# Layer 1 of a two-layer convolution: silu on pairs of units over 128 partitions, residual rows loaded in the layout of the output, and another division of r between VectorE and ScalarE

## The chip, the cores and the metric

The kernel runs on one core of one Trainium2 chip. The metric is the device time of one execution in microseconds; the time before is the median of three runs, and lower is better. A core has TensorE (PE in the profile, its weight loads PEld), VectorE (DVE), ScalarE (ACT), GpSimd (POOL) and SyncE (SP, which here only issues DMAs).

## The reference

The input x has shape (4, 16, 256, 256): four images of 16 channels. Both layers have the form x = x + f(groupnorm(x)).

Layer 0 computes, for every pixel and channel, 25 logits by a 3x3 convolution, a softmax over them, and the sum of the 5x5 neighbourhood weighted by it. The change touches only what it prepares for layer 1.

Layer 1 is a convolution of spline features and of silu, both 3x3:

```python
base_w = base_weight.sum(axis=2)
spl_w = (spline_weight * spline_scaler[..., None]).sum(axis=2)
out = jnp.einsum('bjhwn,ijn->bihw', jax.nn.silu(patches), base_w)
out = out + jnp.einsum('bjhwns,ijns->bihw', bspl, spl_w)
out = out + bias_weight[None, :, None, None]
x = x + out
```

`bspl` are eight cubic B-spline bases of the normalised x. With the distance t of x from the centre of a basis, the kernel computes a basis as the difference of two clamped cubes: r = max(c - t, 0), s = r^2, s*r, and beside it (t - 2c)(c - t/2)^2, which `combine` clamps and adds.

## The kernel before

**Stages.** A prologue of some 110 us normalises the first image and prepares weights. Layer 0 then runs to about 2035 us, and layer 1 takes the rest. Layer 0 leaves its result in DRAM (`x1s`, one row of 256 values after the other for each channel), and layer 1 reads it from there.

**Units.** Layer 1 works through 64 units: 4 images times 16 bands of 16 image rows (`RU = 16`). For a unit n,

- `load_x(n)` (lines 1027 to 1034) brings 16 rows into one of three buffers `xta`, `xtb`, `xtc`, laid out over 128 partitions as 16 channels times 8 bases: two DMAs of 1 MB each;
- `load_tiles(n)` (line 1040) brings the same x into partitions 64 to 127 of one of three tiles `sla`, `slb`, `slc`: 4 DMAs (one per row offset d of `RD = 4`) to 16 partitions each, in rows of 1 KB;
- `distance`, `inner`, `square`, `cube`, `far`, `cubed`, `combined` (lines 1068 to 1108) make the features in chunks of four rows (`QR = 4`; 128x1024 elements) and write them into `ring`, which holds the rows of two units. `inner` makes r: chunks 0, 1 and 2 on VectorE (line 1079), the last four rows on ScalarE (a Relu, line 1077);
- `silu(n)` (line 1048) reads partitions 64 to 127 of the unit's `sl` tile and writes silu into partitions 0 to 63;
- `outputs(n)` (line 1225) accumulates in PSUM: 12 products (d, e) of `ring` with the spline weights `wt`, then 3 products of the `sl` tile with `ws`. `ws` holds the silu weights for partitions 0 to 63 and an identity for partitions 64 to 127, so the raw x of the upper half adds the residual;
- `put` (line 1210) adds the bias while it copies the PSUM sum to an SBUF tile `yo` on VectorE, and `store` issues two DMAs of 128 KB to the output. Both are two units behind (`LAG1 = 2`): in `features(n)` they handle unit n-2.

**Order.** `features(n)` (line 1168) writes out the order of the work by hand: it interleaves the later features of unit n with the earlier ones of unit n+1 (`ahead_of(n + 1)`) and with `distance` of unit n+2. `in_order` then chains all instructions of an engine in the order in which the code emits them, SP's DMAs too; nothing is reordered. In the steady stage the orders of one unit are, from `put` to `put`:

- DVE: put, cubed 2, cubed 3, combined 2, combined 3 (unit n), then inner 0 (n+2), cubed 0 (n+1), inner 1, combined 0, cubed 1, inner 2, combined 1, and the next put;
- ACT: far 3, distance, far 0, far 1, silu, square of chunks 0 and 1, relu, far 2, square of two rows, and the next far 3;
- SP: two stores (wait for put), load_x(n+3) (2 DMAs), a halo copy inside `ring` every other unit, load_tiles(n+2) (4 DMAs).

`far` writes a PSUM tile of a pool of two, so a `far` waits for the `combined` of two chunks before. Every second unit below 32 also runs one step of `scales`, a chain of small instructions for the normalisation of images 2 and 3.

Of the kernel before, what the change touches and what calls it, by code (L numbers as in the profile page):

```python
# [11 lines left out]
F32 = mybir.dt.float32  # L12
# [22 lines left out]
def conv_preact_kernel(  # L35
# [72 lines left out]
    for k, d in enumerate((0, RD - 1)):  # L108
        nc.vector.reduce_sum(inside[:, k : k + 1], ident[:, d:P:RD], AX.X)
    nc.vector.tensor_scalar(inside, inside, -1.0, 1.0, ALU.mult, ALU.add)  # L110
# [17 lines left out]

    ws = const.tile([P, 3, RT, C], F32, name="ws")
    nc.gpsimd.memset(ws, 0.0)  # L130
    for r in range(RT):
        nc.sync.dma_start(ws[P // 2 + r + 1 : P : RD, 1, r], ident[0:C, 0:C])

# [327 lines left out]
    with tc.tile_pool(name="prep0", bufs=2) as prep, tc.tile_pool(  # L461
# [98 lines left out]
        def prepare1():  # L560
# [18 lines left out]
            for r in range(RT):  # L579
                nc.vector.tensor_copy(  # L580
                    wt[:, r : r + 3, :, r, :], wcp.rearrange("p (d e o) -> p d e o", d=3, e=3)
                )
                for d in range(3):
                    nc.sync.dma_start(
                        ws[r + d : P // 2 : RD, :, r, :],
                        wb1[d * C : (d + 1) * C].rearrange("p (e o) -> p e o", e=3),
                    )

# [386 lines left out]
    def layer1(arm, last, marks, seeds):  # L975
# [5 lines left out]
        with ExitStack() as pools:  # L981
# [12 lines left out]
            xt0 = fixed("xta", XT)  # L994
            r1a, r1b = fixed("r1a", [P, 3 * QR, W])[0], fixed("r1b", [P, QR + 1, W], 2)
            s1a = fixed("s1a", XT)
# [5 lines left out]
            xtt = xt0 + xt1 + fixed("xtc", XT)  # L1002
            sl += fixed("slb", SL) + fixed("slc", SL)
            yop = pool("yo", 3)
            ps2 = pool("ps2", 2, space=PSUM)
# [34 lines left out]
            def load_tiles(n):  # L1040
                b, u = units[n]
                for d in range(RD):
                    nc.sync.dma_start(
                        sl[n % 3][P // 2 + d : P : RD, :, 1 : W + 1],
                        rows(x1s[b], [[CP, C], [RT * W, RU // RT], [1, W]], u * RU + d),
                    )

            def silu(n):
                b, u = units[n]
                q0, q1 = 1 if u == 0 else 0, RU // RT - (1 if u == NU - 1 else 0)  # L1050
                for a, z, k in ((0, q0, 4), (q0, q1, 0), (q1, RU // RT, 6)):
                    if a < z:
                        nc.scalar.activation(
                            sl[n % 3][0 : P // 2, a:z, 1 : W + 1],
                            sl[n % 3][P // 2 :, a:z, 1 : W + 1], AF.Silu,
                            scale=sc[b][k][P // 2 :], bias=sc[b][k + 1][P // 2 :],
                        )

            def r1(n, a, z):
                lo = span(units[n][1])[0]  # L1060
                t, o = (r1a, lo) if a - lo < 3 * QR else (r1b[n % 2], lo + 3 * QR)
                return t[:, a - o : z - o]
# [11 lines left out]
            def inner(n, a, z, act):  # L1074
                r, t = r1(n, a, z), xs(n, a, z)
                if act:
                    nc.scalar.activation(r, t, AF.Relu, bias=cb, scale=-1.0)  # L1077
                else:
                    nc.vector.scalar_tensor_tensor(  # L1079
                        r, t, cb, pc.unsqueeze(2).to_broadcast([P, z - a, W]), ALU.min, ALU.subtract  # L1080
                    )
# [21 lines left out]
            def combined(n, c, ps):  # L1103
                a, z = cuts(units[n][1])[c]
                combine(
                    ring[:, place(n) + a : place(n) + z, 1 : W + 1], ps, s1(n, a, z),
                    ALU.subtract if n > 0 and c < 3 else ALU.add,
                )

            def start_unit():  # L1110
                cs = cuts(0)
                for v in cs[:3]:
                    distance(0, *v)
                    inner(0, *v, True)
                    square(0, *v)
                    cube(0, v)
                    if v == cs[1]:
                        early = newest(POOLE).name
                v = cs[3][0], cs[-1][1]
                distance(0, *v)  # L1120
                inner(0, *v, True)
                square(0, *v)
                cube(0, *cs[3:])
                return early

            def ahead_of(n):
                cs = cuts(units[n][1])
                lo = cs[0][0]
                tail = cs[3][0], cs[-1][1]
                yield  # L1130
                inner(n, *cs[0], False)
                yield
                inner(n, *cs[1], False)
                yield
                square(n, lo, cs[1][1])
                cube(n, *cs[:2])
                inner(n, *tail, True)
                yield
                inner(n, *cs[2], False)
                yield  # L1140
                square(n, cs[2][0], lo + SQ)
                square_late(n, lo + SQ, cs[2][1])
                square_late(n, *tail)
                cube(n, *cs[2:])
                yield

            def first_features(ps):
# [11 lines left out]
                next(pre)  # L1159
                ps.append(far(0, 4))  # L1160
                silu(0)
                next(pre)
# [47 lines left out]
            def put(lag=LAG1):  # L1210
                if len(waiting) >= lag:
                    b, u, yp = waiting[0]
                    yo = yop.tile([P, 2, W], F32, name=f"yo_{b}_{u}{arm}", tag="yo")
                    nc.vector.tensor_scalar(yo, yp, bias_sb, None, ALU.add)
                    waiting[0] = b, u, yo
# [9 lines left out]
            def outputs(n):  # L1225
# [12 lines left out]
                for e in range(3):  # L1238
                    for t in range(NT):
                        nc.tensor.matmul(  # L1240
                            yp[t * M : (t + 1) * M],
                            lhsT=ws[:, e].rearrange("p r o -> p (r o)"),
                            rhs=sl[n % 3][:, t : t + NT + 1 : NT, e : e + W],
                            start=False, stop=e == 2,
                        )
# [7 lines left out]
            load_x(1)  # L1253
            load_tiles(0)
            load_x(2)
            load_tiles(1)
            def sides(t):
# [11 lines left out]
            halo(0)  # L1269
            for t in sl:  # L1270
                sides(t)
            first_far = [far(0, 0), far(0, 1)]
            first_rest = len(nc.cur_bb.bb.instructions)
            for n in range(len(units)):
                if n % 2:
                    next(more, None)
                if n > 0:
                    halo(n)
                    if n + 1 < len(units) and n > 0:
                        load_tiles(n + 1)  # L1280
                if n == 0:
# [3 lines left out]
                if n == 1:  # L1285
                    behind(seeds[2], newest(DVEE).name)
                if n + 3 < len(units):
                    load_x(n + 3)
                outputs(n)
            for _ in range(LAG1):  # L1290
                put(1)
                store(1)
# [61 lines left out]
```

## Time and profile before

| | us |
|---|---|
| median of 3 runs | 2939.93 (2938.02 to 2942.46) |
| the profiled execution's own time | 2938.03 |
| its span (first to last instruction) | 2936.3 |

| stage, us from the start of the span | length | PE | DVE | ACT | POOL | DMA share |
|---|---|---|---|---|---|---|
| 0 to 100 (prologue) | 100 | 46.24 | 71.22 | 69.85 | 35.41 | 0.93 |
| 1000 to 1500 (layer 0) | 500 | 477.78 | 495.56 | 330.35 | 488.35 | 0.85 |
| 2040 to 2100 (start of layer 1) | 60 | 51.02 | 55.31 | 54.82 | 50.59 | 0.65 |
| 2200 to 2800 (layer 1) | 600 | 594.86 | 597.35 | 594.08 | 545.67 | 0.70 |
| 2880 to 2936.3 (end) | 56.3 | 48.76 | 34.11 | 24.92 | 24.37 | 0.17 |

The columns of the engines are busy microseconds in the stage. A matmul's end is modelled, so a busy PE need not be one at its peak. DMA share is the mean busy share of the 16 DMA engines.

In a timeline a line gives start, duration, engine, line of the code, operation, output and input tiles, shape and count. Consecutive instructions of one engine overlap in their records by some 0.1 us, so the difference of two starts is the better price of an instruction. A strip of the DMA view cuts a window into 40 equal slices: the upper row is the busy share in tenths, the lower what was moved in GB/s.

The put of unit n-2 is a convenient mark of a unit. It starts at 2079.46 us in the first unit that has one, and 59 units later at 2883.95 us; most units take 13.52 us from put to put, the first of each image about 15.

### The profile page before, as it was taken

How to read it: one execution, taken by the hardware profiler on the slowest of the kernel's cores; microseconds unless marked ns; L12 is line 12 of the kernel's file. 1: busy time of each engine (PE TensorE's matmuls, PEld its weight loads, DVE VectorE, ACT ScalarE, POOL GpSimd, SP SyncE). 2: the span in 40 equal slices, each digit the busy share in tenths (PEclk: the TensorE clock that was granted, in tenths of full speed). 3: DMA queues.
4: the chain of work that ended last, by engine and by line, in shares of the span. 5: the costliest groups of instructions: out<-in, count | busy, mean ns of one | idle time of the engine just before them, and what ended most of it. 6: DMA issues, size and time to landing. Idle time of an engine off the chain costs nothing.

```text
span 2936.3 us, 40887 instructions
## 1 busy us (share of the span) xinstructions
PE 2742.2 (93%) x14282; PEld 1486.3 (51%) x14282; DVE 2840.3 (97%) x1866; ACT 2161.5 (74%) x2764; POOL 2703.7 (92%) x1116
## 2 busy tenths in 40 slices
PE   4699999999999899999999989996999999999998
PEld 3466656666666566656656656663323323222222
DVE  7599999999999999999999999998999999999996
ACT  6566876667766567667555554657999999999995
POOL 4399999999999999999999999999899999899895
PEclk7799999999999999999999999997999999999999
DMA  9988999889889788898886766766666767767663
GB/s 277 260 238 230 261 258 254 239 219 252 242 231 242 204 221 232 231 251 226 223 216 168 210 177 174 195 179 208 200 220 217 228 213 225 226 211 233 216 218 99
DMA packets 385736, 647.60 MB, mean 221 GB/s; under 512 B 41842, under 2 KB 250180, under 8 KB 369652
## 3 DMA queue, kind: packets, MB, share of 16 engines
q1 hardware_dynamic: 321556, 609.73, 73.4%
q10 hardware_dynamic: 61920, 31.46, 4.0%
q0 software_dynamic: 2048, 3.72, 0.5%
q8 instruction: 117, 1.92, 0.3%
q14 instruction: 95, 0.78, 0.1%
HBM read 516.18 MB, written 121.15 MB: 217 GB/s over the span
## 4 chain that ended last, share of the span: by engine, by line
DVE 39%; ACT 21%; PE 20%; DMA 8%; issue 7%; POOL 3%; SPq 2%; ACTq 0%; DVEq 0%; POOLq 0%
DVE nd L771 32%; PE lg L922 12%; ACT s L170 4%; PE lg L926 3%; PE yp L1231 3%; ACT xtc L1070 2%; ACT xtb L1070 2%; ACT xta L1070 2%; POOL e L950 2%; ACT s1a L1084 2%; DMA an<-hsl 2%; ACT s1b L1084 2%; ACT r1b L1077 1%; DMA am<-hst 1%; DVE ring L176 1%
## 5 line engine op out<-in xcount | busy, mean ns | idle before, releaser
L950 POOL TENSOR_TENSOR e<-e,u 128x1600 f32<-128x1600 f32 x512 | 1789.0, 3547 | 49.7 <-ACT e L945 49.4
L922 PE MATMUL lg<-wm,am 128*128 128x400 f32 x4096 | 1732.9, 504 | 74.3 <-ACT e L945 35.7
L771 DVE TENSOR_REDUCE nd<-e 128x128 f32<-128x3200 f32 x512 | 1762.9, 3494 | 30.3 <-POOL e L950 29.9
L926 PE MATMUL lg<-wn,an 97*128 97x400 f32 x2048 | 1342.5, 656 | 14.3 <-DMA an<-hsl 13.8
L945 ACT ACTIVATE e<-lg 128x800 f32<-128x800 f32 x1024 | 833.5, 838 | 577.2 <-PE lg L926 332.4
L922 PEld LDWEIGHTS lg<-wm,am 128*128 128x128 f32 x4096 | 763.5, 192 | 386.9 <-ACT e L945 64.4
L1231 PE MATMUL yp<-ring,wt 128*32 128x512 f32 x6144 | 763.5, 595 | 38.9 <-DVE ring L176 34.9
L926 PEld LDWEIGHTS lg<-wn,an 97*128 97x128 f32 x2048 | 387.4, 189 | 333.8 <-DMA an<-hsl 25.3
L1231 PEld LDWEIGHTS yp<-ring,wt 128*32 128x32 f32 x6144 | 223.1, 109 | 528.6 <-issue 421.9
L1091 POOL TENSOR_TENSOR s1a<-s1a,r1a 128x1024 f32<-128x1024 f32 x96 | 228.7, 2398 | 43.9 <-ACT s1a L1084 43.9
L1091 POOL TENSOR_TENSOR s1b<-s1b,r1a 128x1024 f32<-128x1024 f32 x96 | 228.9, 2400 | 35.1 <-ACT s1b L1084 35.1
L176 DVE SCALAR_TENSOR_TENSOR ring<-s,s1a 128x1024 f32<-128x1024 f32 x132 | 158.7, 1233 | 0.9
L825 ACT ACTIVATE z<-xc,nrm 128x256 f32<-128x256 f32 x240 | 144.0, 600 | 18.0 <-POOL xc L805 13.8
L176 DVE SCALAR_TENSOR_TENSOR ring<-s,s1b 128x1024 f32<-128x1024 f32 (+1 forms) x128 | 155.6, 1246 | 0.3
L173 DVE SCALAR_TENSOR_TENSOR s<-xta,cb,s 128x1024 f32<-128x1024 f32 (+2 forms) x90 | 113.6, 1293 | 0.7 <-ACT s L170 0.4
L173 DVE SCALAR_TENSOR_TENSOR s<-xtb,cb,s 128x1024 f32<-128x1024 f32 (+2 forms) x85 | 108.5, 1309 | 0.5 <-ACT s L170 0.4
L173 DVE SCALAR_TENSOR_TENSOR s<-xtc,cb,s 128x1024 f32<-128x1024 f32 (+2 forms) x85 | 108.2, 1305 | 0.4 <-ACT s L170 0.4
L170 ACT ACTIVATE s<-xta,cb 128x1024 f32<-128x1024 f32 (+2 forms) x90 | 96.5, 1086 | 7.4 <-DVE ring L176 7.0
L785 ACT ACTIVATE r<-nd 128x512 f32<-128x512 f32 x64 | 38.3, 598 | 78.9 <-DVE nd L799 78.9
L170 ACT ACTIVATE s<-xtc,cb 128x1024 f32<-128x1024 f32 (+2 forms) x85 | 91.8, 1094 | 1.3 <-DVE ring L176 0.7
L170 ACT ACTIVATE s<-xtb,cb 128x1024 f32<-128x1024 f32 (+2 forms) x85 | 91.8, 1093 | 0.8 <-DVE ring L176 0.4
L1079 DVE SCALAR_TENSOR_TENSOR r1a<-xtc,cb,pc 128x1024 f32<-128x1024 f32 x63 | 82.7, 1312 | 4.5 <-issue 4.5
(211 smaller groups left out, 2434.0 us busy)
## 6 DMA issues: line engine op xcount, KB each, us to landing
am<-hst SPq DMA_DIRECT2D x512, 194.6 KB
u<-hs SPq DMA_DIRECT2D x320, 288.0 KB
an<-hsl SPq DMA_DIRECT2D x512, 129.8 KB
xta<-x1s SPq DMA_DIRECT2D x40, 1024.0 KB
xtb<-x1s SPq DMA_DIRECT2D x40, 1024.0 KB
xtc<-x1s SPq DMA_DIRECT2D x40, 1024.0 KB
am<-hst SPq DMA_DIRECT2D x256, 129.8 KB
x1s<-xc ACTq DMA_DIRECT2D x30, 1024.0 KB
```

What stands on the lines that cost most here:

```text
L170: nc.scalar.activation(s, t, AF.Square, scale=-0.5, bias=cb)
L173: nc.vector.scalar_tensor_tensor(p, t, cb2, s, ALU.subtract, ALU.mult)
L176: nc.vector.scalar_tensor_tensor(f, p, 0.0, q, ALU.min, op)
L771: nc.vector.tensor_reduce(nd[:, :, :, j : j + JG].rearrange("p t c j -> p t j c"), e.rearrange("p t j m c d -> p t j c m d"), AX.XY, ALU.add,)
L825: nc.scalar.activation(z, v, f, scale=nrm[b][:, 0, g : g + 1], bias=nrm[b][:, 1, g : g + 1], accum_out=st1[b][:, t, g, columns_of(n) : col ...
L922: nc.tensor.matmul(lg[:, i, :NL], lhsT=am[:, o : o + P], rhs=wm.rearrange("p m c d -> p (m c d)"), start=True, stop=False,)
L926: nc.tensor.matmul(lg[:, i, :NL], lhsT=an[:, o : o + P], rhs=wn.rearrange("p m c d -> p (m c d)"), start=False, stop=True,)
L945: nc.scalar.activation(ev, lg[:, :, :NL], AF.Exp)
L950: nc.gpsimd.tensor_tensor(e[:, 1].rearrange("p j m c d -> p j (m c) d"), e[:, 0].rearrange("p j m c d -> p j (m c) d"), uv, ALU.mult,)
L1070: nc.scalar.activation(xs(n, a, z), xs(n, a, z), AF.Abs, scale=sc[b][2], bias=sc[b][3])
L1091: nc.gpsimd.tensor_tensor(s1(n, a, z), s1(n, a, z), r1(n, a, z), ALU.mult)
L1231: nc.tensor.matmul(yp[t * M : (t + 1) * M], lhsT=wt[:, d, e].rearrange("p r o -> p (r o)"), rhs=ring[:, r0 + t * RT + d : r0 + t * RT + d ...
```

## The change

It has four parts.

1. **silu of two units at a time.** Units 2m and 2m+1 share one `sl` tile: the even unit's x goes into partitions 0 to 63, the odd one's into 64 to 127. silu runs in place on all 128 partitions, in two halves of 1024 elements: the first in `features(2m-1)`, the second in `features(2m)`. `ws` becomes two sets of weights, one with zeros for the upper half and one with zeros for the lower; `outputs(n)` takes set n % 2. The identity in `ws` is gone.
2. **The residual in the layout of the output.** A new `load_rows(n)` loads the unit's 16 rows of x into the `yo` tile (two DMAs of 128 KB, each partition 1 KB), and `put` becomes one `scalar_tensor_tensor`: PSUM sum + bias + that tile, in place. The pool of `yo` has 4 buffers instead of 3.
3. **The order on SP.** After `features(n)`: load_tiles(n+3), load_x(n+3), load_rows(n-1), and then the next unit's halo. `put` in `features(n+1)` reads the rows that are loaded here.
4. **r for 10 rows on VectorE and the rest on ScalarE.** `inner` on VectorE makes 4 + 4 + 2 rows, the Relu on ScalarE six instead of four. r on VectorE changes its sign, so `combine` always adds. GpSimd's products follow the new cut: six rows squared in one instruction instead of two and four, and one chunk's cube in two halves.

In the prologue the two DMAs of the identity into `ws` (line 132) go, and the six DMAs of the silu weights (line 584) become twelve.

```diff
@@ prologue
-    ws = const.tile([P, 3, RT, C], F32, name="ws")
+    ws = const.tile([P, 2, 3, RT, C], F32, name="ws")
     nc.gpsimd.memset(ws, 0.0)
-    for r in range(RT):
-        nc.sync.dma_start(ws[P // 2 + r + 1 : P : RD, 1, r], ident[0:C, 0:C])
...
                 for d in range(3):
-                    nc.sync.dma_start(
-                        ws[r + d : P // 2 : RD, :, r, :],
-                        wb1[d * C : (d + 1) * C].rearrange("p (e o) -> p e o", e=3),
-                    )
+                    for h in range(2):
+                        nc.sync.dma_start(
+                            ws[h * (P // 2) + r + d : (h + 1) * (P // 2) : RD, h, :, r, :],
+                            wb1[d * C : (d + 1) * C].rearrange("p (e o) -> p e o", e=3),
+                        )
@@ layer1
-            r1a, r1b = fixed("r1a", [P, 3 * QR, W])[0], fixed("r1b", [P, QR + 1, W], 2)
+            r1a, r1b = fixed("r1a", [P, SQ, W])[0], fixed("r1b", [P, RU + 1 - SQ, W], 2)
...
-            yop = pool("yo", 3)
+            yop = pool("yo", 4)
...
             def load_tiles(n):
                 b, u = units[n]
+                h = n % 2 * (P // 2)
                 for d in range(RD):
                     nc.sync.dma_start(
-                        sl[n % 3][P // 2 + d : P : RD, :, 1 : W + 1],
+                        sl[n // 2 % 3][h + d : h + P // 2 : RD, :, 1 : W + 1],
                         rows(x1s[b], [[CP, C], [RT * W, RU // RT], [1, W]], u * RU + d),
                     )
 
+            def load_rows(n):
+                b, u = units[n]
+                t = yop.tile([P, 2, W], F32, name=f"yo_{b}_{u}{arm}", tag="yo")
+                for g in range(2):
+                    nc.sync.dma_start(
+                        t[:, g], rows(x1s[b], [[W, 8], [CP, C], [1, W]], u * RU + 8 * g + 1)
+                    )
+                kept_rows.append(t)
+
             def silu(n):
-                b, u = units[n]
-                q0, q1 = 1 if u == 0 else 0, RU // RT - (1 if u == NU - 1 else 0)
-                for a, z, k in ((0, q0, 4), (q0, q1, 0), (q1, RU // RT, 6)):
-                    if a < z:
-                        nc.scalar.activation(
-                            sl[n % 3][0 : P // 2, a:z, 1 : W + 1],
-                            sl[n % 3][P // 2 :, a:z, 1 : W + 1], AF.Silu,
-                            scale=sc[b][k][P // 2 :], bias=sc[b][k + 1][P // 2 :],
-                        )
+                m = (n + 1) // 2
+                if m >= len(units) // 2:
+                    return
+                b, u = units[2 * m]
+                q0, q1 = (0, RU // RT // 2) if n % 2 else (RU // RT // 2, RU // RT)
+                parts = [(q0, q1, 0)]
...
+                for a, z, k in parts:
+                    t = sl[m % 3][:, a:z, 1 : W + 1]
+                    nc.scalar.activation(t, t, AF.Silu, scale=sc[b][k], bias=sc[b][k + 1])
...
             def ahead_of(n):
...
                 square(n, lo, cs[1][1])
                 cube(n, *cs[:2])
-                inner(n, *tail, True)
+                inner(n, mid, hi, True)
                 yield
-                inner(n, *cs[2], False)
+                inner(n, cs[2][0], mid, False)
                 yield
-                square(n, cs[2][0], lo + SQ)
-                square_late(n, lo + SQ, cs[2][1])
-                square_late(n, *tail)
-                cube(n, *cs[2:])
+                square(n, cs[2][0], mid)
+                square_late(n, mid, hi)
+                cube_late(n)
                 yield
...
             def put(lag=LAG1):
                 if len(waiting) >= lag:
                     b, u, yp = waiting[0]
-                    yo = yop.tile([P, 2, W], F32, name=f"yo_{b}_{u}{arm}", tag="yo")
-                    nc.vector.tensor_scalar(yo, yp, bias_sb, None, ALU.add)
+                    yo = kept_rows.pop(0)
+                    nc.vector.scalar_tensor_tensor(yo, yp, bias_sb, yo, ALU.add, ALU.add)
                     waiting[0] = b, u, yo
...
             for n in range(len(units)):
...
                 if n > 0:
                     halo(n)
-                    if n + 1 < len(units) and n > 0:
-                        load_tiles(n + 1)
...
                 if n + 3 < len(units):
+                    load_tiles(n + 3)
                     load_x(n + 3)
...
+                if n > 0:
+                    load_rows(n - 1)
                 outputs(n)
+            load_rows(len(units) - 1)
             for _ in range(LAG1):
                 put(1)
                 store(1)
```

## The prediction

> **What bounds the kernel now.** The change works in layer 1, so I looked first at the busy times of a stage in its middle (PE, PEld, DVE, ACT, POOL, then clock, DMA share and GB/s).
>
> ```profile
> 2200.00:2800.00 600.00, 594.86 (x5278) 183.40 (x5274) 597.35 (x550) 594.08 (x406) 545.67 (x278) 1.00 0.70 221
> ```
>
> Three engines are above 99%, GpSimd has a tenth free, the DMA engines three tenths. Next, the timelines of ACT and DVE in one ordinary unit, whose put starts at 2571.11 and whose next put at 2584.63: 13.52 us.
>
> ```profile
> 2572.35 3.79 ACT L1070 ACTIVATE xtb<-xtb,q 128x4096 f32<-128x4096 f32 x1
> 2576.05 2.13 ACT L170 ACTIVATE s<-xta,cb 128x1024 f32<-128x1024 f32 x2
> 2578.20 2.10 ACT L1053 ACTIVATE sla<-sla,q 64x2048 f32<-64x2048 f32 x1
> 2580.33 1.91 ACT L1084 ACTIVATE s1a<-r1a 128x2048 f32<-128x2048 f32 x1
> 2582.15 1.13 ACT L1077 ACTIVATE r1b<-xtb,cb 128x1024 f32<-128x1024 f32 x1
> 2583.19 1.10 ACT L170 ACTIVATE s<-xta,cb 128x1024 f32<-128x1024 f32 x1
> 2584.23 0.62 ACT L1084 ACTIVATE s1a<-r1a 128x512 f32<-128x512 f32 x1
> 2584.82 1.12 ACT L170 ACTIVATE s<-xta,cb 128x1024 f32<-128x1024 f32 x1
> ```
>
> ```profile
> 2577.60 1.35 DVE L173 SCALAR_TENSOR_TENSOR s<-xta,cb,s 128x1024 f32<-128x1024 f32 x1
> 2578.79 1.34 DVE L1079 SCALAR_TENSOR_TENSOR r1a<-xtb,cb,pc 128x1024 f32<-128x1024 f32 x1
> 2584.63 0.81 DVE L1214 TENSOR_SCALAR yo<-yp,bias_sb 128x512 f32<-128x512 f32 x1
> ```
>
> ACT has no gap: its prices from start to start are distance 3.70, far 0 and 1 2.15, silu 2.13, square 1.82, relu 1.04, far 2 1.04, second square 0.59, far 3 1.06, together 13.53. DVE has none either: put 0.66, four cubed and three inner at 1.19, four combined at 1.13, together 13.51. PE needs 30 groups of weight loads at 0.43, 12.9 us, and waits for the ring for the rest.
>
> SP and the transfers come last, since the change moves them. SP's queue and the DMA strip (0.35 us a slice) for the unit whose put starts at 2406.62:
>
> ```profile
> 2407.46 1.36 SPq L1221 DMA_DIRECT2D out_dram<-yo  x2
> 2408.93 1.50 SPq L1031 DMA_DIRECT2D xtc<-x1s  x2
> 2411.70 2.55 SPq L1043 DMA_DIRECT2D slb<-x1s  x4
> ```
>
> ```profile
> DMA  0000044449946999899999989899999851100000
> GB/s 18 0 0 0 0 79 149 167 114 260 301 99 211 398 421 445 374 445 421 398 445 468 445 374 445 337 316 272 196 240 187 146 94 26 26 9 0 0 0 0
> ```
>
> All transfers start when put has ended, and come one behind the other: stores at four tenths, then 2 MB of x, then the tiles at some 224 GB/s, done near 2419.4. DMA is on no critical path here: what it loads is read a unit later or more.
>
> From 2120 to 2880 us SP waited for put in 56 units, 6.3 us each:
>
> ```profile
> SPq L1221 <- DVE yo L1214: 351.0, 56, 8.7
> ```
>
> **What the Trainium skill says.** "DMA: Bandwidth & Descriptors", section "Queues, rings and completion order": each DMA engine takes descriptors in ring order. The strip agrees: tiles issued 2.8 us after x land after it. Same page, "Why a DMA increments its semaphore by 16 and not by 1": a transfer uses the largest number up to 16 of engines that divides the slowest dimension of both sides, and is done when all have landed. The stores have 8 rows there, and their slices are at four tenths, as eight engines would give; the new row loads have the same 8. "ScalarE: Activation LUTs", "What ACT_TABLE_LOAD costs": 186 ns + 0.833 ns an element, 93 ns more for each per-partition scale or bias. For the silu of 2048 that is 2.08; the trace has 2.10.
>
> **The change part by part**, T being the start of a put.
>
> *ACT.* silu of 1024 elements: 0.186 + 2 x 0.093 + 0.853 = 1.23 (estimate by that page), about 1.25 from start to start instead of 2.13: -0.88. The relu of 1536: the squares cost 1.82 for 2048 elements and 0.59 for 512, so 0.41 for 512, which gives 1.04 + 0.41 = 1.45; the page's 0.833 gives 1.47, which I take: +0.43. Sum 13.08.
>
> *DVE.* The third inner falls from 1024 to 512 elements, 1.19 to 0.66 (put has 512 and costs 0.66): -0.53. put gets a second operand; the same operation at 512 elements in layer 0 (line 795) is 0.60 from start to start, 0.71 long, so -0.06 to +0.05: I take 0. Sum 12.98.
>
> *A dependence loop that the silu used to cover.* The first square needs inner 1, which follows cubed 0, which needs far 0. From the start of square: 1.82 + 1.47 (relu) + 1.04 + 0.59 + 1.06 + 3.70 to the start of far 0, 1.15 to its result, cubed 0 1.19, inner 1 1.31 to its result: 13.33. Before, with a relu of 1.04, 12.90, below the 13.52. So ACT waits 0.25 us ahead of square: of 0.45 gained on ACT only 0.19 arrives. A unit can't be faster than 13.33.
>
> *GpSimd.* One fewer square instruction (about -0.15), one more cube (about +0.15), 12.4 us a unit: hidden by its tenth. *PE.* The same number of matmuls, floor 12.9: hidden.
>
> *SP and the transfers.* The row loads of unit n-1 come last in SP's order and are needed by the very next put, and the first entry of the order, the stores, waits for the put before. So from put to put runs a chain: put 0.84 to the first store's issue; stores and gap to T+2.31; four tile issues 2.55, T+4.88; then x and the rows. Before, x's issue was at T+2.31: the tiles now stand ahead of it. From x's issue to the end of x and tiles the strip shows 10.5 us. Take off the tiles (0.52 MB at 224 GB/s, 2.34), add the rows (0.26 MB on half the engines; the stores' three full slices average 143 GB/s, so 1.83): 9.99, landing at T+14.9. That is the upper end. The lower comes from the start of layer 1, where tiles and x run on an otherwise idle queue (0.3 us a slice):
>
> ```profile
> 2030.47 2.51 SPq L1043 DMA_DIRECT2D sla<-x1s  x4
> 2033.02 1.25 SPq L1031 DMA_DIRECT2D xtc<-x1s  x2
> ```
>
> ```profile
> DMA  0000003857766599348999998999999994200056
> GB/s 0 0 0 0 0 0 92 273 130 195 205 229 222 164 348 246 82 137 300 382 437 410 437 437 355 382 410 410 410 437 437 437 410 191 109 27 0 0 82 201
> ```
>
> x is through 7.4 to 7.8 us after its issue. With rows at the tiles' rate on all engines (1.2) that is T+13.5, with 1.83 T+14.1. Bounds 13.5 and 14.9; I take 14.3. This exceeds 13.33, and put waits about a microsecond in each unit. Behind it stand DVE's cubed and combined, for these PE and ACT, and SP's stores, with which the next round starts: the wait isn't caught up.
>
> The tile loads land at T+6.5 (in the strip of the start 1.6 us after the last issue's end); the silu that needs the odd unit's comes at T+7.1 and has 0.25 us of wait behind it. Hidden, with 0.6 to spare; a microsecond late would cost 0.2 a unit (every other one). SP has 10 issues, 7.8 us, and had 6 us of waiting a unit.
>
> *Prologue and start.* Six more weight DMAs at 1.19 us (7.14 for six) put 7.1 us before the stores of normalised rows in SP's queue; two DMAs, 2.76 us, are gone from its beginning, ahead of 2 MB loads that bound the first 28 us. ACT, busy all through 60 to 80, covers part. -3 to +5; I take 0. The tables and silu at the start of layer 1 are three pieces instead of two, +0.3. The end is set by the last two units' matmuls after the last features: unchanged.
>
> **Sum.** From the put at 2079.46 to the one at 2883.95 lie 59 units that load x and rows. Before 804.5. After: 56 at 14.3 and the three first units of an image, which DVE makes long, at 14.6: 844.6. The steps of scales (up to 0.6) vanish in put's wait. +40.1, +0.3 and -0.2 for the unit after: about +40 on the profiled execution's 2938.0, 2978. The median was 1.9 above that execution: 2980.
>
> **Rivals.** *Other side: rows in time.* If x and rows are through by T+13.33, the loop above decides: 59 x (13.52 - 13.33) = 11 us less, 2929. For it: x's packets at the start of layer 1 ran faster, and eight engines may finish early. Against: it takes the lower bound of x and 0.6 us or less for rows. The switch is at a landing of T+13.33 for gain, T+13.6 for break-even with the mean unit. *Full gain:* if also square doesn't wait (far 0 earlier), ACT and DVE give 13.08: -26, 2914. Against it: each engine's order is chained. *Transfers worse than the bound:* one late DMA engine ends every transfer; at T+15.2 56 units give +94, 3034. *No difference:* landing at T+13.5 to 13.7.
>
> **Chances.** Within 0.2% (6 us) is what a measurement of this kernel can't tell from none. Rows late, landing 13.7 to 14.9: 0.73, 2946 to 3015, most of it beyond +0.2%. Rows in time 0.13, full gain 0.03: faster 0.16. Landing around 13.6: 0.05, and a little of the first: same 0.07. Worse: 0.06. Slower 0.77. The range 2932 to 3018 takes in the late case and the upper half of the case in time.
>
> **What would show it.** Right: put (a SCALAR_TENSOR_TENSOR from yp) idle before it by about 1 us, released by the DMA of yo; put-to-put 14.0 to 14.6; silu 1.2 us long, 128x1024; DMA share in the middle stage near 0.72. Wrong: DVE idle before cubed 0 and ACT before square, with put not waiting, means rows in time; ACT idle before silu means the tiles are late; a first exp of layer 0 later than 118 us by several us means the prologue pays.

## The result and the profile after

The changed kernel takes 3065.37 us (median of four runs, 3052.67 to 3073.75) against 2939.98 for the kernel before in the same session: a ratio of 1.0422, 95% interval 1.0384 to 1.0461. It is slower, as forecast, and by three times as much: +125 us where +40 was forecast, and beyond the range's end of 3018.

The profiled executions took 3052.67 and 2938.03, 114.6 apart. From put to put the 59 units of the main loop now take 15.54 us in the mean instead of 13.64; 59 x 1.905 is 112.4, and the first put is 2.5 later (2081.96 for 2079.46). The end after the last of these units is 0.6 shorter. So nearly all of it lies where the prediction put it. (The changed kernel's median is 12.7 above its profiled execution, the fastest of its four runs, which are 21 us apart; the four runs of the kernel before are 4.4 apart. That the waits described below differ from run to run would explain it, but only one execution was profiled.)

The busy times of the middle stage (PE, PEld, DVE, ACT, POOL, clock, DMA share, GB/s):

```profile
2200.00:2800.00 600.00, 552.11 (x4638) 162.59 (x4630) 505.10 (x488) 507.87 (x357) 478.98 (x246) 0.99 0.63 210
```

All the engines that stood at 594 to 597 of 600 have fallen to 505 to 552, and the DMA engines from 0.70 to 0.63: everything waits, and no engine is the bound. The group of the put, from the page of the changed kernel, says for what (busy and mean ns, then the idle time before it and what ended most of that):

```profile
L1235 DVE SCALAR_TENSOR_TENSOR yo<-yp,bias_sb,yo 128x512 f32<-128x512 f32 x64 | 48.1, 751 | 161.3 <-DMA yo<-x1s 133.8
```

The operation itself costs nothing more (751 ns, 0.66 from start to start as before), but DVE stands idle 161.3 us ahead of it, 133.8 of them for the row loads. The waits of DVE and then of PE, between 2150 and 2950 us (total, times, longest), show that this is DVE's only wait on a transfer, and what it does to others:

```profile
DVE yo L1235 <- DMA yo<-x1s: 110.2, 47, 4.6
DVE yo L1235 <- PE yp L1252: 10.1, 4, 2.9
```

```profile
PE yp L1252 <- DVE ring L175: 59.0, 42, 2.5
```

47 of the puts wait, 2.3 us each. Cubed and combined stand behind the put on DVE, and PE waits for the ring rows that combined writes.

SP's queue for one unit of average length, whose put starts at 2766.05, and the put that ends it:

```profile
2766.83 1.34 SPq L1242 DMA_DIRECT2D out_dram<-yo  x2
2768.23 2.53 SPq L1045 DMA_DIRECT2D sla<-x1s  x4
2770.80 1.25 SPq L1032 DMA_DIRECT2D xtb<-x1s  x2
2772.09 1.96 SPq L1054 DMA_DIRECT2D yo<-x1s  x2
```

```profile
2781.58 0.75 DVE L1235 SCALAR_TENSOR_TENSOR yo<-yp,bias_sb,yo 128x512 f32<-128x512 f32 x1 [2.44 <-DMA yo<-x1s]
```

And its DMA strip from 2766.05 to 2782.05 (0.4 us a slice):

```profile
DMA  0000044457786769638998999999995551000000
GB/s 0 0 0 0 0 67 143 151 133 207 254 261 169 231 200 330 128 102 307 389 471 369 451 389 410 389 471 410 389 376 182 187 195 64 23 23 26 10 0 0
```

The chain of the prediction is there: stores issued 0.78 us after put's start, tiles at T+2.18, x at T+4.75 (4.88 was forecast), rows at T+6.04. In the strip stores and tiles run to about T+7, x to T+12, then the rows for three slices at five tenths, and then a tail: four slices with only 10 to 26 GB/s, at less than a tenth, until T+15.2 at the latest. The records of single DMA packets in this unit show what it is. The last 8 KB packet of x ends at T+13.64; from there on come, apart from markers of 4 bytes, only row packets of 1 KB, one behind the other, 0.043 us apart, the last from T+14.96 to T+15.00. That is one engine, which came from x to the rows late and does its eighth of them (32 packets of 256, 1.4 us) while the others have ended. Put needs all of its rows, so it waits for that engine, and starts at T+15.53, 0.53 after the packet. Over all 59 units the picture is less pure: in 27 the last row packet ends 1.37 to 1.45 us after the last of x, as it does here; in 17 it ends sooner after it, in 15 later.

### The profile page after: what moved, and what is told of

It reads as the page before. It is cut to its first block, busy times and chain, and to the rows that moved or that the text cites. A ratio compares the mean times of both kernels' runs of the same rounds, so it can differ in the third digit from the quotient of the medians.

```text
span 3050.8 us, 40925 instructions
## 1 busy us (share of the span) xinstructions
PE 2790.5 (91%) x14282; PEld 1488.5 (49%) x14282; DVE 2808.4 (92%) x1866; ACT 2138.5 (70%) x2764; POOL 2701.5 (89%) x1117
## 4 chain that ended last, share of the span: by engine, by line
DVE 41%; DMA 20%; PE 19%; ACT 5%; SPq 5%; issue 5%; POOL 4%; DVEq 0%; POOLq 0%; ACTq 0%
DVE nd L771 30%; DMA yo<-x1s 14%; PE lg L922 12%; PE lg L926 3%; DVE s L172 3%; POOL e L950 2%; PE yp L1252 2%; DMA am<-hst 2%; DVE ring L175 2%; DMA x1s<-xc 2%; DMA an<-hsl 2%; SPq L1045 1%; DVE yo L1235 1%; SPq L1032 1%; ACT s L169 1%
## 5 line engine op out<-in xcount | busy, mean ns | idle before, releaser
L1252 PE MATMUL yp<-ring,wt 128*32 128x512 f32 x6144 | 811.0, 603 | 108.0 <-DVE ring L175 102.2
L1109 POOL TENSOR_TENSOR s1a<-s1a,r1a 128x1024 f32<-128x1024 f32 (+1 forms) x96 | 192.8, 2024 | 118.1 <-ACT s1a L1102 118.1
L1109 POOL TENSOR_TENSOR s1b<-s1b,r1a 128x1024 f32<-128x1024 f32 (+1 forms) x96 | 193.0, 2026 | 80.6 <-ACT s1b L1102 80.6
L1235 DVE SCALAR_TENSOR_TENSOR yo<-yp,bias_sb,yo 128x512 f32<-128x512 f32 x64 | 48.1, 751 | 161.3 <-DMA yo<-x1s 133.8
L1109 POOL TENSOR_TENSOR s1a<-s1a,r1b 128x512 f32<-128x512 f32 (+2 forms) x68 | 118.9, 1773 | 0.0
L1109 POOL TENSOR_TENSOR s1b<-s1b,r1b 128x512 f32<-128x512 f32 x64 | 113.6, 1799 | 0.0
L1102 ACT ACTIVATE s1b<-r1a 128x2048 f32<-128x2048 f32 x64 | 81.0, 1266 | 39.9 <-DVE r1a L1096 39.9
```

Source lines behind the costliest of these rows:

```text
L1102: nc.scalar.activation(s1(n, a, z), r1(n, a, z), AF.Square)
L1109: nc.gpsimd.tensor_tensor(s1(n, a, z), s1(n, a, z), r1(n, a, z), ALU.mult)
L1252: nc.tensor.matmul(yp[t * M : (t + 1) * M], lhsT=wt[:, d, e].rearrange("p r o -> p (r o)"), rhs=ring[:, r0 + t * RT + d : r0 + t * RT + d ...
```

## The experiments

Times are medians; ratios are to the kernel before, on the same chip in the same session. "Put to put" is the mean of the 59 units of the profiled execution.

| kernel | us | ratio, 95% interval | put to put |
|---|---|---|---|
| changed | 3065.4 | 1.0422 (1.0384 to 1.0461) | 15.54 |
| e1 rows one unit earlier | 2937.4 | 0.9989 (0.9980 to 0.9998) | 13.62 |
| e2 order tiles, rows, x | 2990.3 | 1.0174 (1.0152 to 1.0196) | 14.47 |
| e3 no rows | 2935.8 | 0.9988 (0.9981 to 0.9995) | 13.61 |
| e4 rows part alone on the kernel before | 2948.2 | 1.0034 (1.0022 to 1.0045) | 13.71 |
| e7 no ring copies | 3048.5 | 1.0385 (1.0362 to 1.0407) | 15.45 |
| e8 rows loaded twice | 3155.3 | 1.0729 (1.0712 to 1.0745) | 17.20 |
| e11 order x, tiles, rows | 3058.8 | 1.0410 (1.0392 to 1.0429) | 15.46 |
| e12 order x, rows, tiles | 2955.0 | 1.0051 (1.0031 to 1.0070) | 13.84 |
| e5 e1 + inner 1 first | 2931.2 | 0.9976 (0.9966 to 0.9986) | 13.44 |
| e6 e5 + first ring copy early | 2928.4 | 0.9964 (0.9950 to 0.9977) | 13.49 |
| e9 e6 + order x, rows, tiles | 2924.9 | 0.9950 (0.9937 to 0.9963) | 13.37 |
| e10 e9 + cubed 1 first | 2912.3 | 0.9906 (0.9891 to 0.9920) | 13.19 |
| e13 e10 + start reordered | 2906.1 | 0.9885 (0.9870 to 0.9900) | 13.08 |
| e14 e1 + rows later at the start | 2941.1 | 1.0003 (0.9995 to 1.0012) | 13.54 |

The theory was the prediction's chain from put to put. Its rivals: that the 16.8 MB of rows slow the queue wherever they stand (traffic), or that the rest of the change costs the time (rest).

**e1: rows one unit earlier.**

```diff
-                if n > 0:
-                    load_rows(n - 1)
+                load_rows(n)
                 outputs(n)
-            load_rows(len(units) - 1)
```

> One edit to the changed kernel: the rows of a unit are loaded one unit earlier in SP's order (rows of n, not of n-1), so the put that needs them comes a whole unit after the put behind which they are issued. Chain theory (the changed kernel is slow because from put to put runs a chain stores, tiles, x, rows, put): put no longer waits for a DMA, the unit falls from 15.54 to the dependence loop of 13.33 us, 2929 us. Traffic theory (16.8 MB more in 1 KB rows, on eight engines of sixteen, slow the queue whatever their place): the same bytes in the same queue, no less than 3040. Rest theory (silu on 128 partitions, the r split or the early tiles cost it): no less than 3000.

All of the loss is gone with the same bytes in the same queue: 2937.4. That is above the 2929 of the chain theory and far below the 3000 and 3040 of the others. DVE's waits between 2150 and 2850 no longer have a put or a DMA in them:

```profile
DVE r1a L1096 <- issue: 8.5, 27, 0.8
DVE r1a L1096 <- POOL s1b L1105: 3.1, 11, 0.6
DVE s L172 <- ACT s L169: 1.9, 4, 0.5
DVE r1a L1096 <- POOL s1a L1105: 0.5, 2, 0.2
```

Traffic and rest both fall; the chain from put to put is shown to be the cause. But the unit is 13.47, not 13.33, and the kernel gains 2 us, not 11. Two things are open: why the chain was longer than forecast, and where the gain is.

**e3: no rows.**

```diff
-                    yo = kept_rows.pop(0)
-                    nc.vector.scalar_tensor_tensor(yo, yp, bias_sb, yo, ALU.add, ALU.add)
+                    yo = yop.tile([P, 2, W], F32, name=f"yo_{b}_{u}{arm}", tag="yo")
+                    nc.vector.tensor_scalar(yo, yp, bias_sb, None, ALU.add)
...
-                    load_rows(n - 1)
```

> The changed kernel without its residual rows: put adds the bias alone and no rows are loaded, so the residual is left out of the output of layer 1; silu, r split, tiles and weights stay as changed. Chain theory and traffic theory: 2929 us, with a unit of 13.33. Rest theory: no less than 3000. The difference from the kernel with rows one unit earlier is what the rows themselves cost, apart from their place: 0 to 10 us by the chain theory.

2935.8: without rows nothing of the loss is left, so silu, tiles, r and weights don't make it by themselves (the tiles' part in it follows with e11 and e12). Its interval overlaps that of e1, so rows that are loaded early cost next to nothing. Its ordinary unit is 13.47 as well, so that length isn't due to the rows.

**e2: rows ahead of x.**

```diff
                     load_tiles(n + 3)
+                if n > 0:
+                    load_rows(n - 1)
+                if n + 3 < len(units):
                     load_x(n + 3)
```

> One edit to the changed kernel: SP's order in a unit is tiles, rows, x instead of tiles, x, rows; which put needs which rows stays. Chain theory: the rows land some 8 us after the put behind which they are issued, not 15; put doesn't wait, the unit is 13.33, 2929 us. Traffic theory: no less than 3040. If only the completion of a row load is slow (whatever is ahead of it), put would still wait a little, 2950 to 3000.

Neither theory's number. Put waits for no transfer, as the chain theory says, but the wait came back elsewhere. ACT's waits on x, 2150 to 2850:

```profile
ACT xta L1087 <- DMA xta<-x1s: 15.8, 11, 2.8
...
ACT xtc L1087 <- DMA xtc<-x1s: 13.9, 10, 3.3
...
ACT xtb L1087 <- DMA xtb<-x1s: 10.5, 8, 2.5
```

29 distances wait, 40.2 us together. The packet records have x's last packet at T+16.3 in the mean here; in a unit of 13.47 distance would read it near T+15.4. In e1, where x has only stores and tiles ahead of it, its last packet comes at T+13.4. So x has a slack of some 2 us less the time from packet to reader, which the prediction ("what it loads is read a unit later or more") had not measured, and the rows ahead of it use it up.

**e4: the rows part alone, on the kernel before.** Put adds rows that are loaded behind x, instead of the identity weights that gave the residual (put and weights as in the change, not shown again); the tiles stay behind the rows.

```diff
                     load_x(n + 3)
+                if n > 0:
+                    load_rows(n - 1)
                 outputs(n)
+            load_rows(len(units) - 1)
```

> The kernel before with the rows part alone: put adds rows that are loaded last in SP's order behind x, needed by the next put; silu of one unit on 64 partitions, the r split and the place of the tiles (behind x) stay as before. Chain theory: x is issued some 2.4 us earlier than in the changed kernel, so the rows land near T+13.1 instead of T+15.5, below the 13.52 that ACT sets: 2935 to 2955 us, and the tiles ahead of x are then what makes the rows late. Traffic theory: no less than 3040. If the rows take their time behind any x, not through the tiles: 15 us a unit, about 3030.

2948.2, within the 2935 to 2955 of the chain theory. The late rows come from two parts together: rows at the end, and tiles ahead of them.

**e11 and e12: x first.** The changed kernel with x issued 2.4 us earlier; the tiles of one unit later follow it, ahead of the rows in e11, behind them in e12. e11:

```diff
-                    load_tiles(n + 3)
                     load_x(n + 3)
+                if n + 4 < len(units):
+                    load_tiles(n + 4)
                 if n == 1:
                     sides(sl[2])
                 if n > 0:
                     load_rows(n - 1)
```

> The changed kernel with SP's order x, tiles, rows instead of tiles, x, rows (the tiles of one unit later, so that they are still in time); rows are still last and needed by the next put. Issue theory (as the prediction put it, it is the four tile issues ahead of x, 2.55 us, that push the landing): rows land 2.4 us earlier, the unit falls to 13.5, about 2940. Queue theory (what counts is that the tiles' bytes pass ahead of the rows, in whichever order): in the kernel before the tiles' last packet behind x came at T+13.1 to 13.5; rows 0.9 to 1.6 more and 0.64 from the last packet to put give units of 14.7 to 15.6, 3010 to 3070.

3058.8, 15.46 from put to put, and put waits as before (2150 to 2950):

```profile
DVE yo L1235 <- DMA yo<-x1s: 92.4, 40, 3.8
```

x's issue moved from T+4.75 to T+2.23, and nothing came of it: the issue theory falls. The four tile issues ahead of x were not what made the rows late; the bytes of the tiles ahead of the rows were. In e12 the two last lines of this diff's additions stand below `load_rows(n - 1)`:

> The changed kernel with SP's order x, rows, tiles (the tiles of one unit later); the rows are still needed by the next put. Both theories: no tiles are ahead of the rows, x is issued 2.4 us earlier, the rows are through near T+13.1, so put waits only where a transfer runs late: units of 13.5 to 13.7, 2940 to 2955. If units stay above 14.5, x and rows alone are too slow for a chain from put to put, and the tiles had no part in it.

2955.0: with the tiles behind them, the rows are nearly in time, 24.5 us of waits in the same window against 92.4 with the tiles ahead:

```profile
DVE yo L1235 <- DMA yo<-x1s: 24.5, 27, 1.7
```

The two kernels differ in nothing else.

**e7: no ring copies.** In the changed kernel every second unit has a copy of two ring rows (258 KB) in SP's queue, and those units were the longer ones.

```diff
-                elif r0 == 0:
+                elif r0 == 0 and n < 4:
                     nc.sync.dma_start(ring[:, 0:2, :], ring[:, 2 * RU : 2 * RU + 2, :])
```

> The changed kernel without the copies of two ring rows that start every second unit (258 KB on SP's queue, issued behind the rows), from the second one on: the first two rows of the ring then hold old values, so part of the output of layer 1 is left wrong. In the changed kernel the 26 units in which such a copy runs last 16.03, the others 15.10. Copy theory (its packets run beside the end of x and the rows and delay the landing): all units 15.1, some 25 us less, 3040. Parity theory (odd and even units differ through the halves of the silu or the two square buffers): alternation and time stay, 3065.

The mean unit fell by 0.09, not by the 0.44 from 15.54 to 15.10. The 26 units that had a copy did become shorter (16.01 to 15.27), but the others longer (15.17 to 15.59). By the times alone, the medians are 17 us apart, 0.3 a unit, and the intervals of the two kernels overlap. The copies shape the alternation and are not the missing microsecond; neither theory holds as written.

**e8: rows twice.**

```diff
                 if n > 0:
+                    load_rows(n - 1, True)   # into a tile of its own
                     load_rows(n - 1)
```

> The changed kernel with each unit's rows loaded twice, first into a tile that nothing reads, then as before: 0.26 MB more in the chain, at its end. It sizes the term for the rows. At the rate of eight engines (143 GB/s, 1.83 us, the price in the upper end of the prediction) the unit grows to 17.4, 3170 to 3175; at the rate of all sixteen (224 GB/s, 1.17) to 16.7, 3132 to 3135; if rows cost what stood between the last packet of x and theirs (0.9 to 1.0) to 16.5, 3118 to 3125.

17.20 from put to put, +1.65, and 3155.3, +90 on the changed kernel's median (1.6 for each of 56 units). So 0.26 MB more at the end of the chain costs 1.6, nearest to the price of eight engines (1.83, of which it is 0.2 short). It is more than what stands between the last packets of x and of the rows in the changed kernel: the two overlap. (That is 1.2 in the mean of the 59 units; the 0.9 to 1.0 of the expectation come out when packets of 8 and 16 KB from the queues that fetch instructions are counted as x.)

**e5: where e1's 13.47 comes from.** Its ACT and DVE around one unit:

```profile
2603.28 3.79 ACT L1087 ACTIVATE xta<-xta,q 128x4096 f32<-128x4096 f32 x1
...
2610.87 1.91 ACT L1102 ACTIVATE s1a<-r1a 128x2048 f32<-128x2048 f32 x1 [0.59 <-DVE r1a L1096]
```

```profile
2607.17 1.28 DVE L1096 SCALAR_TENSOR_TENSOR r1a<-xta,cb,pc 128x1024 f32<-128x1024 f32 x1 [0.25 <-issue]
2608.37 1.28 DVE L172 SCALAR_TENSOR_TENSOR s<-xtc,cb,s 128x1024 f32<-128x1024 f32 x1
2609.56 1.28 DVE L1096 SCALAR_TENSOR_TENSOR r1a<-xta,cb,pc 128x1024 f32<-128x1024 f32 x1
```

The distance of the next unit ends at 2607.07; inner 0 starts 0.1 later, and cubed 0 stands behind it on DVE. So the loop enters DVE through inner 0, at 2607.17 + 1.20, and not through far 0, whose result (2606.97 + 1.15 = 2608.12) is there a quarter of a microsecond earlier. e5 puts inner 1 ahead of cubed 0:

```diff
                 next(pre, None)
-                cubed(n, 0, ps[0])
                 next(pre, None)
+                cubed(n, 0, ps[0])
                 combined(n, 0, ps[0])
```

> The kernel with the rows one unit earlier, and one more edit: on DVE the second inner of the next unit (1024 elements) stands ahead of the first cubed. In that kernel the unit is 13.47, and its timeline shows a loop: distance 3.79 and 0.10 to inner 0, inner 0 1.20, cubed 0 1.19, inner 1 1.31, then square 1.82, relu 1.47, far 1.04, second square 0.52, far 1.04. Loop theory: without the 1.19 of cubed 0 in it ACT's own sum sets the unit, 12.9 to 13.1; 56 units less by 0.4 to 0.55 give 2905 to 2917. PE theory (PE, busy for 595 of 600 us, has become the bound): the unit stays at 13.47, 2937. DMA theory (x can't land in a shorter unit, with tiles ahead of it): distance waits for x and the unit stays above 13.2, 2920 or more.

2931.2, where the loop theory had at most 2917; only the DMA theory's "2920 or more" holds it. By the times alone, the intervals of e1 and e5 just overlap; the trace is clearer. The ordinary unit fell to 13.20, and PE, which could have been the bound, followed, so the PE theory falls. The loop was real, but what came after it was not ACT's sum: DVE binds in the ordinary unit (e10 bears this out), and many units were longer than 13.20 because ACT waited for tiles and x, as the DMA theory has it.

**e6, e9, e10, e13: a version that beats both.** e6 issues the first ring copy earlier:

> The kernel with rows one unit earlier and inner 1 ahead of cubed 0, and the first ring copy (halo of unit 2) ahead of the tiles and x of unit 4 in SP's order instead of behind them and two row loads. The kernel with rows earlier lost 4.4 us in its first unit, where PE waited 4.6 for that copy. If the copy's place is why, 3 to 5 us less than without this edit: 2901 to 2913 with the loop theory. If the first unit is long through x of unit 3 (ACT waited 4.4 for it) and not through the copy, no gain.

2928.4; the intervals of e5 and e6 overlap, and the mean unit didn't fall. The first unit was 16.25 for 17.26, but 18.27 and 19.40 in e9 and e10, which keep this edit: the copy's place is not what makes it long. e9 gives every load a whole unit, in the order x, rows, tiles:

```diff
-                    load_tiles(n + 3)
                     load_x(n + 3)
...
                 load_rows(n)
+                if n + 4 < len(units):
+                    load_tiles(n + 4)
```

> The kernel with rows one unit earlier, inner 1 ahead of cubed 0 and the first ring copy early, and SP's order in a unit now x, rows, tiles, with the tiles of one unit later, so that all three are read a unit after they are issued. In the kernel with tiles first the shortest unit is 13.20 (DVE), the mean 13.44 to 13.49, and ACT waits for tiles and x in many. If these waits are what lengthens the units: mean near 13.3, 2912 to 2922. If the queue has no more to give (DMA share 0.72): no change, 2928.

2924.9, 3 us above what the first theory gave and 3 below the second; the intervals of e6 and e9 overlap. In the trace the waits for transfers are gone from ACT and DVE between 2150 and 2850, and the ordinary unit is 13.20 throughout, but the first unit is 18.27. e10 puts cubed 1 ahead of combined 0:

```diff
-                combined(n, 0, ps[0])
                 cubed(n, 1, ps[1])
+                combined(n, 0, ps[0])
```

> As the kernel with tiles last, with cubed 1 ahead of combined 0 on DVE, which takes away the 0.12 us between cubed 0 and the combined that reads it. DVE's own sum is 12.98, ACT's 12.86, PE's groups 12.9. If that gap is what stands between 12.98 and 13.20: unit 13.05 to 13.1, 6 to 9 us less than with tiles last. If far 2 then waits for the later combined 0, which frees its PSUM buffer: no gain or a loss.

2912.3, 12.6 less where 6 to 9 were expected: the unit is 12.99, DVE's own sum of 12.98, and the middle stage has no gap left on PE or DVE:

```profile
2200.00:2800.00 600.00, 599.64 (x5513) 213.00 (x5508) 598.63 (x573) 594.04 (x424) 570.01 (x290) 1.00 0.81 250
```

What was left was the first unit, 19.40 us. SP's and ACT's waits from 2070 to 2098 in e10:

```profile
SPq L1054 <- DVE mv L843: 19.1, 1, 19.1
```

```profile
ACT xtb L1087 <- DMA xtb<-x1s: 6.6, 1, 6.6
```

The first row load sits 19 us on SP until layer 0 frees its buffer, with the x of unit 4 behind it. e13 issues that x first:

```diff
                 if n + 3 < len(units):
                     load_x(n + 3)
+                if n == 1:
+                    halo(2)
+                    load_rows(0)
+                    load_tiles(4)
...
-                load_rows(n)
-                if n + 4 < len(units):
-                    load_tiles(n + 4)
+                if n > 0:
+                    load_rows(n)
+                    if n + 4 < len(units):
+                        load_tiles(n + 4)
```

> The kernel with tiles last and cubed 1 first, and in the start of layer 1 the x of unit 4 issued ahead of the row and tile loads of the first units, which wait on SP 19 us until layer 0 frees their buffers. In the kernel without this edit ACT waited 6.6 us for that x and the first unit was 19.40. If the order on SP is why: first unit 13.5 to 14.5, 4 to 6 us less, 2906 to 2909. If the queue is simply full there: no change, 2912.

2906.1, 6.2 less, and a first unit of 12.99: a little more than expected. This kernel is 1.15% faster than the one before (0.9885, 0.9870 to 0.9900).

**e14: the same question on e1 alone.** There the tile loads, which also wait for layer 0, stay ahead of that x.

```diff
-                load_rows(n)
+                if n > 0:
+                    if n == 1:
+                        load_rows(0)
+                    load_rows(n)
                 outputs(n)
```

> The changed kernel with rows one unit earlier, but in the start of layer 1 the first two row loads stand behind the x of unit 4. With rows one unit earlier the first unit was 17.96 (13.52 before); without rows at all 14.74. If the row loads, waiting on SP for their buffers ahead of that x, are why: first unit near 14.7, 3 us less than with rows one unit earlier, 2932 to 2936. If not: 2937.

2941.1, no gain: a miss. The first unit fell from 17.96 to 12.99, but the first put came at 2088.27 instead of 2082.25, because now it waited 4.4 us for its own rows. SP waits 19.6 us with the tile load instead. The time at the start moved ahead of the mark by which it had been counted; of the kernels tried, only e13, which takes both loads from ahead of x, is without it.

## Why the prediction was wrong

**Right:** the mechanism and its place (put waits for rows that are last in a queue which starts anew behind each put), and that engines made shorter gain nothing while it does. The prices of the operations: silu of 1024 elements 1.24 long (1.23), relu 1.46 from start to start (1.47), third inner 0.66 (0.66), put no dearer. x's issue within 0.15.

**The step that failed is the landing of the rows.** The prediction took T+14.3 between 13.5 and 14.9 and let put start at it. In the packet records of the changed kernel (mean of its 59 units) the rows' last packet ends at T+14.90, and put starts at T+15.54. Two terms were mis-sized:

- *The end of the packets, +0.6.* The upper end, 14.9, was met; choosing below it was wrong. The choice rested on the start of layer 1, where x was through 7.4 to 7.8 us after its issue, with a short tail. In the middle of the stage nine tenths of x were through 7.1 us after its issue, but the last packet came 8.8 after it (8.9 in the kernel before). The rows' own term was fair: 1.83 for the upper end, 1.65 by e8. Instead of a bound from a quiet moment, the strip of the ordinary unit should have been trusted to its last non-zero slice. In the packet records the kernel before ends its 2.9 MB at T+13.1 in the mean of the units without a ring copy (12.8 was read from the strip of one of them); with 1.65 for rows that is 14.8, and the 33 such units of the changed kernel have 14.56. The 26 with a ring copy, which the prediction's chain doesn't have, are at 15.32. That the mean of both is 14.90 is in part luck.
- *From the last packet to the instruction that waits, +0.65, taken as nothing.* The 59 puts start 0.65 us in the mean after the end of their last row packet (0.54 to 0.80 for eight in ten). For the 54 whose wait the trace puts down to the rows, 0.53 of it passes before the semaphore that tells of the landing, 0.12 from there to put. In e2 34 distances start 0.45 after x's. The Trainium skill has this: "DMA: Bandwidth & Descriptors", section "Anatomy of one DMA — SWDGE (gpsimd) path", puts most of a DMA's fixed cost of about 2 us into the wait for the receipt of its last byte. That page fits its figure to transfers that GpSimd issues; for these, which SP issues, the trace has 0.53 to the semaphore.

14.90 + 0.65 is, but for rounding, the measured 15.54. The rival "transfers worse than the bound" (one late engine ends every transfer, T+15.2, 3034, given 0.06) was nearer to what happened than the likeliest case.

**The reason given was wrong in one point.** The prediction derived the landing from x's issue, pushed by four tile issues. e11 shows that the order of x and tiles makes no difference to the rows behind both. "Issuing engines are not separate DMA queues", on the same page of the skill, says that the time on the issuing sequencer is usually small beside the transfer. Here four issues take 2.55 us of a chain of 15.5, and taking them from ahead of x changed it by 0.08 (15.54 and 15.46), so in this queue that time is hidden behind the transfers. That the upper end was met although its 2.55 for the issues doesn't count is luck too: counted by bytes alone, 12.8 and 1.83 give 14.6.

**The loop of 13.33** was followed through far 0 and cubed 0; it goes through inner 0, which DVE does ahead of cubed 0, and is 13.47. The case "rows in time" was priced at 2929 for that; with rows in time the kernel took 2937.4 (e1): 56 x 0.14 is 8 us of it. The start, priced at +0.3, holds time too: e1's first unit is 17.96 for 13.52, and e13 shows for its own start that loads waiting for layer 0's buffers ahead of x cost some 6 us. How e1's loss divides among its loads was not separated.

**"Hidden, with 0.6 to spare"** for the tiles was also short by the receipt: in the changed kernel silu waits for its tiles (2150 to 2950; the two lines below are two of the three tiles), which does no harm there: DVE waits at no place but put. In e5, where the unit is short, waits on tiles and x are part of why the mean is 13.44 and not 13.20; e9 removed them.

```profile
ACT slb L1074 <- DMA slb<-x1s: 7.2, 7, 1.4
ACT sla L1074 <- DMA sla<-x1s: 6.3, 6, 1.5
```

**The prologue** can't be told apart: layer 1's first loads were issued 2.3 us earlier than before, and spread over 7.7 us among all these kernels, most of which share one prologue.

**Left open:** why the last packet of x comes 1.7 us behind nine tenths of it in the middle of the stage and 0.9 behind at its start. The ring copies are not why: without them (e7) it still comes 8.6 us after x's issue. A part may be instruction fetches: the packet records have, on a queue marked "instruction", a packet of 16 KB about once a unit, some 1.1 us long on one engine. Over the traces of all 16 kernels x's last packet comes 9.16 us after its issue in the 308 units in which such a packet starts within 7 us of the issue, and 8.61 in the 620 others; in the quiet window at the start there is none. No run tests this, and about half a microsecond is the most that it explains. Rows on all sixteen engines, which might halve the late engine's share, weren't tried.

## What to carry to other kernels

A load that is issued behind an event and needed by the next such event closes a loop. Its length here is everything queued ahead of it up to the last packet of the slowest engine, plus the receipt, plus the time back to the event; if that is near the unit, load one unit earlier, at the price of a buffer or none. Reordering within the unit chooses who waits: in e2 it moved the wait to x, in e12 it all but ended it, since the tiles that went last had a whole unit. What is last in a nearly full queue is late, so give each load a whole unit, and look for loads that sit in an in-order queue waiting for a buffer ahead of one that is urgent.

## What the runs showed that was not expected

- The order of x and tiles ahead of the rows had no effect: 15.54 and 15.46 from put to put (e11), although x was issued 2.5 us earlier.
- One late engine at the end of a transfer shows in the strip as slices of 10 to 26 GB/s at less than a tenth, easily read as nothing; in the unit shown such slices last 1.6 us, and everything waits for them.
- A DMA's end in the strip is not when its reader starts: 0.65 us (DVE, rows) and 0.45 us (ACT, x) lie between.
- The DMA engines carried 0.81 of their time in e10 with hardly a wait on a transfer, and at 0.63 in the changed kernel the time hung on one of their transfers: the share says little where a transfer is on a loop.
- An edit of DVE's order alone (e10) gave 12.6 us, more than the 11 us that the prediction gave to the whole change at the loop's 13.33.
